# A four-layer graph network: the attention turned by VectorE and a DRAM scratch, dots against a row in PSUM, layer 3's statistics on ScalarE

## The chip, the core and the metric

The kernel runs on one core of a Trainium2 chip. The metric is device time in microseconds (us), the median of several runs. A profile of one further execution shows every instruction. The engines are TensorE (PE; PEld is its weight load), VectorE (DVE), ScalarE (ACT), GpSimd (POOL) and SyncE (SP), which issues DMAs.

## What is computed

x is 128 graphs of 128 nodes with 512 features, adj one 128 x 128 matrix with weights for all of them, all in float32. Four layers follow one another; each ends with `x = layernorm(x + layer(x))` over the 512 features.

```python
# layer 0
out = einsum('bnd,do->bno', einsum('nm,bmd->bnd', adj, x), W0) + bias
# layer 1: q, k, v = x Wq^T, x Wk^T, x Wv^T
rel = adj.T * einsum('bnd,bmd->bnm', q, k)
out = einsum('bnm,bmd->bnd', rel / norm(rel, axis=2), v)
# layer 2: h = x W2, s1 = h a[:512], s2 = h a[512:]
e = leaky_relu(s1[:, :, None] + s2[:, None, :], 0.2) * adj
out = elu(einsum('bij,bjf->bif', softmax(e, axis=2), h) + beta * h)
# layer 3: A = adj x, C = adj x + b
out = max(relu(A[:, :, None, :] + (C - A)[:, :, :, None]), axis=-1)
```

In layer 3 C - A is b for every node, so the layer's output is one number per node, relu(max over features of A + b), which is added to all of that node's features.

## The kernel before, in words

The 128 graphs are worked on in 32 groups of four (`G`, `NG`). Nodes lie on the partitions, so one graph is a tile of 128 x 512. All constants stay in SBUF: `m_qk` is Wq^T Wk, `wa` holds W2 a1 and W2 a2 as two rows spread over all partitions (so that s1 and s2 are dots of x with these rows), `beta_i` is beta times the identity matrix.

**The four large products** (y in layer 0, m and v in layer 1, z in layer 2) are done by a Strassen-Winograd scheme of seven block products instead of eight. `left_factors` makes four sums of blocks of the left matrix on POOL (`s_y`, `s_x`, `s_z`; two of the four overwrite a block where `keep` is 0). `product` emits the seven steps in `ORDER = (1, 2, 6, 5, 7, 3, 4)`; each step is four matmuls of 256 columns that accumulate in one of three PSUM regions r0, r1, r2 (`REGION`). After each step `out(i)` copies (ACT) or adds (DVE) the region to its block of the result. Step 2 writes r1, which out(2) reads; step 5 begins r2. In the y product all seven outs are DVE additions onto x.

**Other PE work of a group**: aggregation of y (`p_y`, four graphs), scores (`p_rel`), attention of layer 1 (`p_o`), spread of the dots (`p_s`), transposes of the attention of layer 2 (`p_eT`), gathering of layer 2 (`p_z`), layer 3's aggregation (`p_a`, called widen).

**Layer 2's attention**: `spread` turns the dots d into rows in PSUM; `leaky` (two DVE instructions) makes e; `weighted` multiplies by adj (POOL); `greatest` takes the maximum (DVE); `exps` are four exponentials with sums (ACT); `divide` takes the reciprocal (DVE) and multiplies (POOL); `turn_att` are four PE transposes; `with_beta` adds beta_i while it copies from PSUM (DVE); `gather` multiplies x by the result. In layer 1 the turned relT and, from the third group on, xT are made otherwise: DVE turns 32 x 32 blocks and DMAs move the blocks within SBUF.

**Order.** Every piece is emitted with a number, and all pieces are sorted by it; each engine then executes its instructions in that order, waiting where data or a buffer is not ready, and runs ahead of the numbers where they are. A group's numbers are those of `TABLE` plus 28 per group, so that four groups are in work at a time; one unit (a slot) is 2.48 us. `LAST` replaces the numbers of the last three groups, `FIRST` some of the first two. Within one period of 28 slots (numbers modulo 28) PE does the m product of one group among the aggregations of the next, then the spread (5.6) of the group before, the y product (7 to 13, with `out` 0.72 after each step) among the scores, v among the gathers, and z among the attention of layer 1 and the widen of an older group.

**Buffers.** [...] four for the tag `ps` (all of `bank()`), four in rotation for the regions r.

## Time and profile before

| what | value |
|---|---|
| median of 10 runs | 2236.58 us (2232.23 to 2244.3) |
| the profiled execution | 2239.64 us, of which 2237.3 are the span from the first instruction to the last |
| PE busy | 2183.0 us, 98% of the span |
| DVE busy | 1797.6 us, 80% |
| ACT, POOL busy | 980.5 and 981.8 us, 44% each |
| DMA engines | 20% busy, 115 MB moved |
| mean granted TensorE clock | 0.996 of full speed |

The profile gives, for groups of equal instructions, engine, operation, output<-inputs, shapes and count, then the busy time and the mean length in ns of one, then the idle time of the engine just before them and what ended it. A matmul in float32 appears as two instructions (passes), a PE transpose as one. Matmuls overlap, so that the length of one is more than the distance from start to start. A line of the waits names who waited for whom, the total in us, how often, and the longest. A line of the timeline gives start, length, engine and instruction; like neighbours are merged (x4). Nearly all lines carry L26, the line of a helper, so that the tile's name tells the place.

### The profile page before, as it was taken

How to read it: one execution, taken by the hardware profiler on the slowest of the kernel's cores; microseconds unless marked ns; L12 is line 12 of the kernel's file. 1: busy time of each engine (PE TensorE's matmuls, PEld its weight loads, DVE VectorE, ACT ScalarE, POOL GpSimd, SP SyncE). 2: the span in 40 equal slices, each digit the busy share in tenths (PEclk: the TensorE clock that was granted, in tenths of full speed). 3: DMA queues.
4: the chain of work that ended last, by engine and by line, in shares of the span. 5: the costliest groups of instructions: out<-in, count | busy, mean ns of one | idle time of the engine just before them, and what ended most of it. 6: DMA issues, size and time to landing. Idle time of an engine off the chain costs nothing.

```text
span 2237.3 us, 31661 instructions
## 1 busy us (share of the span) xinstructions
PE 2183.0 (98%) x11073; PEld 1842.2 (82%) x11073; DVE 1797.6 (80%) x3534; ACT 980.5 (44%) x1936; POOL 981.8 (44%) x743
## 2 busy tenths in 40 slices
PE   7999999999999999999999999999999999999986
PEld 5888888888888888888888888888888888888863
DVE  4668888878878788888788888788888788887787
ACT  2224443444444444444444444444444444344535
POOL 3434455335455344544344553344553344543331
PEclk9999999999999999999999999999999999999998
DMA  4010222211222201222212222202222202221101
GB/s 166 25 42 12 57 57 62 62 36 32 61 59 62 62 17 50 58 60 62 46 29 55 57 62 62 50 24 56 57 62 62 47 25 56 58 62 43 23 25 56
DMA packets 333293, 115.13 MB, mean 51 GB/s; under 512 B 297424, under 2 KB 297552, under 8 KB 333136
## 3 DMA queue, kind: packets, MB, share of 16 engines
q1 hardware_dynamic: 331936, 110.77, 19.7%
q10 hardware_dynamic: 1200, 2.36, 0.3%
q8 instruction: 88, 1.44, 0.3%
q14 instruction: 69, 0.57, 0.1%
HBM read 39.65 MB, written 33.55 MB: 33 GB/s over the span
## 4 chain that ended last, share of the span: by engine, by line
PE 76%; DVE 19%; issue 3%; POOL 1%; ACT 1%; DMA 0%; DVEq 0%; ACTq 0%; POOLq 0%
PE r_v L26 17%; PE r_y L26 15%; PE r_z L26 14%; PE r_m L26 8%; DVE x L26 6%; DVE scr L26 6%; PE p_z L26 5%; PE p_o L26 5%; PE p_a L26 5%; PE p_rel L26 4%; DVE st L26 2%; PE p_y L26 2%; DVE tT L26 1%; DVE d L26 1%; PE p_m L26 1%
## 5 line engine op out<-in xcount | busy, mean ns | idle before, releaser
L26 ACT ACTIVATE x<-x,nmean,rstd 128x512 f32<-128x512 f32 x512 | 385.7, 807 | 187.6 <-DVE nmean L26 187.5
L26 DVE BATCH_NORM_STATS2 st<-x 128x6 f32<-128x512 f32 x512 | 352.0, 688 | 56.7 <-ACT x L26 47.9
L26 DVE SCALAR_TENSOR_TENSOR scr<-x,wa 128x512 f32<-128x512 f32 x256 | 286.3, 1169 | 0.0
L26 POOL TENSOR_TENSOR rstd<-ve,mhalf 128x4 f32<-128x4 f32 (+1 forms) x134 | 145.1, 1083 | 288.7 <-DVE ve L26 282.4
L26 POOL TENSOR_TENSOR x<-x,bias_sb 128x512 f32<-128x512 f32 x128 | 191.7, 1508 | 75.9 <-PE p_y L26 75.1
L26 POOL TENSOR_TENSOR s_x<-xT 128x512 f32<-128x512 f32 x64 | 96.6, 1510 | 259.1 <-DMA xT<-xB 238.5
L26 ACT ACTIVATE x<-x,top 128x512 f32<-128x512 f32 x128 | 92.4, 722 | 229.0 <-DVE top L26 228.8
L26 DVE TENSOR_TENSOR x<-r_y,x 128x512 f32<-128x512 f32 x224 | 151.4, 676 | 25.3 <-PE r_y L26 25.2
L26 ACT COPY c<-r_z 128x512 f32<-128x512 f32 x124 | 71.9, 580 | 221.5 <-PE r_z L26 221.5
L26 ACT COPY yT<-p_y 128x512 f32<-128x512 f32 x128 | 75.2, 587 | 206.0 <-PE p_y L26 206.0
L26 PEld LDWEIGHTS p_y<-adjT,x 128*128 128x128 f32 x1024 | 135.4, 194 | 13.4 <-ACT adjT L26 5.4
L26 DVE SCALAR_TENSOR_TENSOR x<-p_o,rn,x 128x512 f32<-128x512 f32 x128 | 95.9, 749 | 59.9 <-PE p_o L26 56.0
L26 PE MATMUL p_y<-adjT,x 128*128 128x128 f32 x1024 | 136.2, 278 | 6.6 <-ACT adjT L26 5.1
L26 PEld LDWEIGHTS p_z<-eT,x 128*128 128x128 f32 x1024 | 135.3, 193 | 8.4 <-DVE x L26 1.2
L26 DVE SCALAR_TENSOR_TENSOR x<-m,x 128x512 f32<-128x512 f32 x128 | 129.7, 1013 | 13.6 <-DVE x L26 0.9
L26 PEld LDWEIGHTS p_rel<-xT,tT 128*128 128x128 f32 x1024 | 134.1, 191 | 7.4 <-DVE tT L26 0.8
L26 POOL TENSOR_TENSOR s_z<-zT 128x512 f32<-128x512 f32 x31 | 39.3, 1267 | 224.1 <-ACT zT L26 224.1
L26 PE MATMUL p_z<-eT,x 128*128 128x128 f32 x1024 | 136.3, 277 | 0.4 <-DVE x L26 0.4
L26 PE MATMUL p_rel<-xT,tT 128*128 128x128 f32 x1024 | 134.9, 275 | 0.6 <-DVE tT L26 0.6
L26 PE MATMUL p_a<-x,adjT 128*128 128x512 f32 x256 | 131.2, 597 | 3.6 <-ACT x L26 1.9
L26 ACT COPY tT<-r_m 128x512 f32<-128x512 f32 x128 | 75.6, 590 | 133.5 <-PE r_m L26 133.5
L26 PE MATMUL p_o<-v,relT 128*128 128x512 f32 x256 | 130.3, 593 | 0.0
(119 smaller groups left out, 5008.7 us busy)
## 6 DMA issues: line engine op xcount, KB each, us to landing
out_dram<-x SPq DMA_DIRECT2D x128, 256.0 KB, 2.5
x<-in_x_dram SPq DMA_DIRECT2D x31, 1024.0 KB, 5.9
xT<-xB SPq DMA_DIRECT2D x480, 64.0 KB, 2.3
relT<-relB SPq DMA_DIRECT2D x512, 16.0 KB, 1.8
w_sb<-in_L_gnn_weight_dram ACTq DMA_DIRECT2D x1, 1024.0 KB, 6.0
x<-in_x_dram SPq DMA_DIRECT2D x4, 256.0 KB, 7.7
wq_sb<-in_L_gnn_Wq_dram SPq DMA_DIRECT2D x1, 1024.0 KB, 11.9
wk_sb<-in_L_gnn_Wk_dram SPq DMA_DIRECT2D x1, 1024.0 KB, 14.9
```

Of the source, the lines that this page charges most:

```text
L26: return lambda *args, **kw: self.tc.keep_in_program_order(op(*args, **kw))
```

## The change

Seven things are changed. (1) `wa` stays in two PSUM banks, where the PE transposes put it; the two copies to SBUF fall away and the dots read PSUM. (2) To make room, `ps` has three banks instead of four; r0 has two banks of its own, and r1 and r2 share one (`r12`). (3) In groups 0 to 29 `divide` is four DVE instructions that multiply by the reciprocal and add beta_i at once; `turn_blocks` turns 32 x 32 blocks in one DVE instruction, and `move` writes these 256 KB to a DRAM scratch in one DMA and reads them back in four, as eT. The last two groups keep the PE transposes. (4) In layer 3 the sum of squares comes from ACT's squares and the sum from the accumulator of ACT's addition; the ReLU of the maximum is ACT's too; five small DVE instructions make mean and variance. (5) The third and fourth bias addition (POOL) come behind the first two sums of y instead of ahead of them. (6) The third and fourth elu, and layer 3 with them, come some slots later. (7) The numbers around these places are set anew.

```diff
+    psum = ctx.enter_context(tc.tile_pool(name="psum", bufs=1, space=bass.MemoryType.PSUM))
+    dram = ctx.enter_context(tc.tile_pool(name="dram", bufs=2, space=bass.MemoryType.DRAM))
     def bank(name):
+        return psum.tile([P, D], FP, tag="ps", name=name, bufs=3)
...
-    wa = const.tile([P, 2, D], FP)
+    wa = psum.tile([P, 2, D], FP, tag="wa", name="wa")
...
     TABLE = dict(
-        load=[-20], y=row(0.5, 1), bias=row(1.3, 1), y_sums=row(5.2, 0.5), y_w=row(7, 1, 7),
+        load=[-20], y=row(0.5, 1), bias=[4.1, 4.6, 9.1, 9.6],
+        y_sums=[6.8, 7.35, 10.2, 10.75], y_w=row(7, 1, 7),
...
-        residual=row(51.0, 1), dots=row(54.2, 1.1), norm1=[55.2], scale=[58.8],
+        residual=row(51.0, 1), dots=[51.7, 53.8, 54.9, 55.6], norm1=[54.6], scale=[57.2],
...
-        spread=[61.6], leaky=[62.0], weighted=[63.4], greatest=[64.3], exps=[64.4],
-        divide=[65.8], turn_att=[68.6], with_beta=[69.0], gather=row(71.5, 1),
-        z_sums=row(75.3, 0.5), z_w=row(77, 1, 7), exp=[87.5, 88.5, 90.4, 92.0],
-        elu=[87.8, 89.4, 92.8, 93.8], norm2=[95.0], apply2=row(95.7, 0.33),
-        widen=[98.7, 100.0, 103.6, 104.6], top=[99.1, 100.4, 104.0, 105.0],
-        stats3=[99.8, 101.1, 104.7, 105.7], norm3=[106.2], apply3=row(107, 0.33), store=[108.5],
+        spread=[61.6], leaky=[61.6], weighted=[62.3], greatest=[63.0], exps=[63.1],
+        divide=[64.2], turn_att=[68.6], with_beta=[69.0], turn_blocks_2=[64.8], move_2=[64.9], gather=row(71.5, 1),
+        z_sums=row(75.3, 0.5), z_w=row(77, 1, 7), exp=[86.0, 87.0, 96.0, 99.6],
+        elu=[86.4, 87.4, 96.8, 100.3], norm2=[101.4], apply2=row(102.4, 0.33),
+        widen=[104.2, 104.9, 105.6, 106.3], top=[104.7, 105.4, 106.1, 106.8],
+        norm3=[107.4], apply3=row(108.4, 0.33), store=[109.8],
...
             first = i in (1, 2, 5)
             if first:
-                r[where] = psum.tile([P, 2, H], FP, tag="r", name=f"r{where}_{name}")
+                r[where] = psum.tile(
+                    [P, 2, H], FP, tag="r0" if where == 0 else "r12",
+                    name=f"r{where}_{name}", bufs=2 if where == 0 else 1,
+                )
...
         def divide(i):
             rs = small.tile([P, n], FP, tag=f"rs{n}", name=f"rs_{g}_{i}")
             dve.reciprocal(rs, s["sums"][:, i * n : i * n + n])
+            if not late:                       # late = g >= NG - 2
+                for b in range(G):
+                    e = s["e"][:, b, :]
+                    dve.scalar_tensor_tensor(
+                        e, e, rs[:, b : b + 1], beta_i, op0=ALU.mult, op1=ALU.add
+                    )
+                return
...
+        def turn_blocks():
+            s["eB"] = work.tile([P, Q, G, P // Q], FP, tag="eB", name=f"eB_{g}")
+            dve.transpose(
+                s["eB"].rearrange("p q b u -> p b q u"),
+                s["e"].rearrange("p b (q u) -> p b q u", q=Q),
+            )
+
+        def move():
+            m = P // Q
+            blocks = dram.tile([P, Q, G * m], FP, tag="eB", name=f"eBd_{g}")
+            sync.dma_start(blocks, s["eB"].rearrange("p q b u -> p q (b u)"))
+            eT = work.tile([P, Q, G, m], FP, tag="eT", name=f"eT_{g}")
+            for q in range(Q):
+                sync.dma_start(
+                    eT[q * m : (q + 1) * m].rearrange("p a b u -> p a (b u)"),
+                    blocks.rearrange("(a j) q n -> q j a n", a=Q)[q],
+                )
...
+        def squares(b):
+            scr = work.tile([P, D], FP, tag="scr3", name=f"scr3_{g}_{b}")
+            act.activation(scr, x3[g][:, b, :], AF.Square, accum_out=s["sq"][:, b : b + 1])
+
         def top(b):
             dve.tensor_reduce(mx, s["a", b], AX.X, ALU.max)
-            dve.tensor_scalar(tp, mx, b3_sb, 0.0, op0=ALU.add, op1=ALU.max)
-            act.activation(x, x, AF.Identity, bias=tp)
+            act.activation(tp, mx, AF.Relu, bias=b3_sb)
+            act.activation(x, x, AF.Identity, bias=tp, accum_out=s["sum"][:, b : b + 1])
+
+        def spread(i):      # mean, and var = sq/D + EPS - (mean of x before the addition)^2
+            dve.tensor_scalar(s["mean", i], s["sum"][:, sl], -1.0 / D, None, op0=ALU.mult)
+            dve.tensor_tensor(d, s["mean", i], s["top"][:, sl], ALU.add)
+            dve.scalar_tensor_tensor(d, d, -1.0, d, op0=ALU.mult, op1=ALU.mult)
+            dve.tensor_scalar(s["sq"][:, sl], s["sq"][:, sl], 1.0 / D, EPS, op0=ALU.mult, op1=ALU.add)
+            dve.tensor_tensor(d, d, s["sq"][:, sl], ALU.add)
+            pool.tensor_tensor(s["r"][:, sl], d, mhalf[:, sl], ALU.pow)
...
-        each(t["stats3"], lambda b: stats(s, f"3_{g}", b, x3[g][:, b, :]))
-        norm(t["norm3"], t["apply3"], s, f"3_{g}", lambda: x3[g])
+        each(t["norm3"], spread)
```

## The prediction

> **What bounds the kernel now.** I read the page's engine table first, then the chain, then the groups by form on PE and DVE, PE's waits, and last the timeline around one group's attention.

> ```profile
> span 2237.3 us, 31661 instructions
> PE 2183.0 (98%) x11073; PEld 1842.2 (82%) x11073; DVE 1797.6 (80%) x3534; ACT 980.5 (44%) x1936; POOL 981.8 (44%) x743
> PE 76%; DVE 19%; issue 3%; POOL 1%; ACT 1%; DMA 0%; DVEq 0%; ACTq 0%; POOLq 0%
> ```

> TensorE (PE) is busy 98% of the span and carries the chain; VectorE (DVE) at 80% only takes it at the end. So time falls where PE issues less or waits less, and rises where PE waits more. In the timeline the four spread transposes `p_s`, one set per group, start 66.81 us apart in the shortest interval; the 28 intervals between the second group and the thirtieth average 67.75. The shortest is PE without a wait: by start-to-start times a group is 112 matmuls of the products at 2 passes of 0.216 (48.4), 48 of 128 columns at 2 passes of 0.112 (10.7), 8 of 512 columns at 2 passes of 0.429 (6.9) and 8 transposes at 0.109 (0.9), together 66.8. About 0.94 us a group is waiting:

> ```profile
> PE r_m L26 <- DVE tT L26: 8.8, 6, 1.7
> PE r_y L26 <- DVE x L26: 4.8, 18, 0.4
> PE p_eT L26 <- DVE rs L26: 2.2, 2, 1.7
> ```

> All of these are DVE being late, and the groups by form show one reason: an instruction with two SBUF inputs takes 1.0 to 1.2 us in the mean, one with a PSUM input 0.75.

> ```profile
> L26 DVE SCALAR_TENSOR_TENSOR scr<-x,wa 128x512 f32<-128x512 f32 x256 | 286.3, 1169 | 0.0
> L26 DVE SCALAR_TENSOR_TENSOR x<-p_o,rn,x 128x512 f32<-128x512 f32 x128 | 95.9, 749 | 59.9 <-PE p_o L26 56.0
> L26 PE MATMUL p_eT<-ident,e 128*128 128x128 f32 x128 | 20.0, 275 | 2.2 <-DVE rs L26 2.2
> ```

> The first timeline is PE through one attention, the second DVE and POOL at a place where short DVE instructions meet a busy POOL.

> ```profile
> 1199.55 0.60 PE L26 MATMUL p_s<-ident,d 128*128 128x128 f32 x4
> ...
> 1201.72 3.62 PE L26 MATMUL r_y<-w_sb,yT 128*128 128x256 f32 x16
> 1205.17 1.05 PE L26 MATMUL p_rel<-xT,tT 128*128 128x128 f32 x8
> 1206.06 1.89 PE L26 MATMUL r_y<-t,s_y 128*128 128x256 f32 x8
> 1207.79 1.05 PE L26 MATMUL p_rel<-xT,tT 128*128 128x128 f32 x8
> 1208.68 1.89 PE L26 MATMUL r_y<-w_sb,s_y 128*128 128x256 f32 x8
> ```

> ```profile
> 1934.94 1.85 DVE L26 SCALAR_TENSOR_TENSOR d<-mv,wa_sum,d 128x4 f32<-128x4 f32 x2
> 1936.89 1.13 DVE L26 TENSOR_TENSOR d<-d,rstd 128x8 f32<-128x8 f32 x1
> 1932.36 5.64 POOL L26 TENSOR_TENSOR x<-x,bias_sb 128x512 f32<-128x512 f32 x4
> ```

> See in the first: step 5 of the y product (the last line) starts 9.13 us after the spread. In the second, three tiny instructions, 0.17 to 0.21 us elsewhere, take 3.0 us: behind back-to-back POOL instructions of 1.27 us each, one DVE instruction gets through per POOL instruction.

> [...] 0.68 alone and up to 1.75 us beside POOL for `scr<-x,wa`, while `x<-p_o,rn,x` keeps 0.75. [...]

> **The change, part by part.**

> *Attention's transposes.* Groups 0 to 29 lose four PE transposes: 120 x 0.109 = **-13.1 us**, all on the path. With them go the copy with beta (0.67 on DVE) and the POOL division (1.04).

> *Dots, layer 3, elu.* `wa` in PSUM takes 8 dots a group from 1.17 to about 0.75 (-3.4 us DVE); layer 3 drops 4 bn_stats and 4 aggregates (4 x 0.87) and the 0.21 us tops, adding about 1.3 us of small instructions; ACT gains 4 squares, 4 accumulator reads and 4 ReLUs, about 5 us a group (nearest rows: 0.72, 0.19; ReLU of one column not shown, 0.2 to 0.4). ACT was 30.6 of 69.4 us a period, so PE's 66 cover it. If that cover were gone, the cost would be a later x3 and so a later widen: up to 0.5 us a group. DVE, some 5 us lighter a group, and two of four elus moved away from the m product: the waits named above should nearly all go. Of 28 x 0.94 = 26.5 I take **-25** (bounds -12 to -26.5). Fewer PSUM buffers (ps 3, r12 one) make new waits possible; in my order of work the banks are free at least 1 us ahead, but for the one place below.

> *Edges.* The chain's last 40 us are mostly DVE: elu, statistics, tops. The eight bn_stats pairs of the last two groups go (8 x 0.8 = 6.4), their tops' 8 x 0.13 too, and about 2.5 of small norm3 work comes: -5; the first two groups wait for DVE about 4 us at `d` and `tT`: -3. Together **-8** (0 to -12; ACT's extra work at the end could eat it).

> *The scratch.* SP gets one write and four reads more a group. Issues take 0.59 us (relT's median), the store lands in 2.5, xT's 64 KB in 2.3. From the turned blocks: 0.6 + 2.5, then 4 x 0.6 + 2.3 = 7.8 us, in which relT's sixteen issues (and any load behind) wait on SP; they are needed 9 slots later. The gather starts about 21 us after the spread; the blocks are turned at 12.4 (below), eT is there at 20.2 and PE will itself be late by then. Cost 0 (bounds 0 to 1 us a group).

> *The new wait.* This decides. `divide` is now four instructions e = e*rs + beta_i on DVE, both tensors in SBUF, emitted ahead of out(2) of the y product (8.2 against 8.72 in slots). With r12 a single buffer, step 5 (r2) cannot start until out(2) has read r1. Times from the spread's start, durations from the timeline around 1200 us: leaky starts at 0.64, two instructions, to 2.05; POOL's product with adj 2.13 to 3.40; maximum 0.72; four exps 1.65, to 5.80; reciprocal, then the first division asks at about 6.03. POOL meanwhile runs on: two y sums to 5.98, and as the third and fourth bias now stand behind these, bias from 5.94, then bias, sum, sum, each 1.27, to 10.90. By the one-for-one rule the four divisions end near 7.25, 8.5, 9.7 and 10.95. out(2) takes 0.68 more and PE 0.14 to start: 11.82 against 9.13 wanted, **+2.7 us** a group, 30 x 2.7 = **+81**. A 128x128 form of this instruction is not in the trace; its neighbour (`e<-e,rs`) is 0.29 with POOL idle, and four of them without POOL would end at 6.9: the other bound is 0. Queued behind PE's wait are two score blocks, the rest of y, then v; behind the divisions on DVE out(2), the turn and out(6).

> Sum: -13.1 - 25 - 8 + 81 = +35. The profiled execution took 2239.64 (span 2237.3), so 2274.5; it lies 3.1 above the median of the runs, so **2272**.

> **Rivals.**
> 1. *The divisions pass POOL* (two or more per gap, or a short form not held up). Then step 5 waits 0 to 0.6 us and the sum is -46 to -28: 2190 to 2209. For it: in most groups the second of the three `d` instructions slipped through when POOL's next came over 0.1 us late. Against it: here POOL's queue is full. It decides from a wait below 1.5 us a group.
> 2. *The first division gets in ahead of the third bias.* The two requests are 0.09 us apart (6.03 and 5.94). One POOL instruction less: 1.4 us a group, 42 in all, sum -4: 2233, no change.
> 3. *More than I see*: the divisions' wait and also an eT that is late by 1 us: +30, about 2300. The trace shows slack against it.

> **How the numbers follow.** Forecast 0.50, with its own range 2256 to 2287 (wait 2.7 +- 0.3, edges and old waits +- 8); rival 1: 0.34; rival 2: 0.13, split about evenly between the three outcomes; rival 3: 0.03. That gives faster by over 0.2% 0.38, within 0.2% (about 4.5 us, what a measurement of this kernel can tell from no change) 0.05, slower 0.57. Two in ten lie outside 2194 to 2287.

> **What would show it.** In the profile after: four PE transposes fewer in each of 30 groups; `scr<-x,wa` at 0.75; `e<-e,rs,beta_i` near 1.2 us instead of 0.3, one per POOL instruction; a PE wait "r_y <- DVE x" at step 5 of y of some 2.7 us times 30, spreads 69.1 us apart. A division at 0.3 us and spreads below 67 us would prove me wrong; waits of `p_z` for eT would prove rival 3.

## The result and the profile after

The kernel takes 2321.36 us after the change (median of 9 runs, 2317.86 to 2321.76) against 2236.9 before: 1.0375 times as long (95% interval 1.0362 to 1.0387). The direction and the place were forecast; the forecast of 2272 with a range to 2287 was 49 us too low. The profiled span is 2320.8 us, 83.5 more than before.

The page's head, engine table and chain, and then two of PE's waits:

```profile
span 2320.8 us, 32156 instructions
PE 2204.1 (95%) x10953; PEld 1857.4 (80%) x10953; DVE 1661.4 (72%) x3410; ACT 1097.0 (47%) x2446; POOL 866.9 (37%) x713
PE 80%; DVE 11%; ACT 4%; issue 2%; POOL 2%; DMA 0%; ACTq 0%; DVEq 0%
```

```profile
PE r_y L26 <- DVE x L26: 76.5, 30, 2.9
PE r_m L26 <- DVE tT L26: 3.5, 1, 3.5
```

DVE, POOL and the DMAs are not short of time: DVE is 136 us less busy than before. Yet PE has one large new wait (`r_y`), once in each of the 30 groups that divide on DVE. And a second thing stands in the engine table: PE issues 120 instructions fewer and is busy 21 us longer, so some matmuls must have become slower.

The groups by form, first DVE's, then PE's:

```profile
L26 DVE SCALAR_TENSOR_TENSOR scr<-x,wa 128x512 f32<-128x512 f32 x256 | 162.4, 681 | 0.0
L26 DVE SCALAR_TENSOR_TENSOR e<-e,rs,beta_i 128x128 f32<-128x128 f32 x120 | 153.6, 1338 | 1.1
L26 PE MATMUL r_y<-w_sb,s_y 128*128 128x256 f32 x512 | 140.1, 422 | 76.5 <-DVE x L26 76.5
L26 PE MATMUL p_eT<-ident,e 128*128 128x128 f32 x8 | 1.9, 300 | 2.2 <-DVE rs L26 2.2
```

The dots went from 1169 to 681 ns, better than the 0.75 us assumed. The divisions take 1338 ns each, four times the 344 ns that a run below shows where POOL does not hold them. Step 5 of y (`r_y<-w_sb,s_y`, together with step 3, which has the same name) went from 382 ns (in the profile before) to 422 in the mean. One attention in the timeline of after; DVE, POOL and PE one after another:

```profile
1179.31 0.18 DVE L26 RECIPROCAL rs<-sums 128x4 f32<-128x4 f32 x1 [1.06 <-ACT e L26]
1179.52 5.11 DVE L26 SCALAR_TENSOR_TENSOR e<-e,rs,beta_i 128x128 f32<-128x128 f32 x4
1184.56 0.68 DVE L26 TENSOR_TENSOR x<-r_y,x 128x512 f32<-128x512 f32 x1
1179.40 2.54 POOL L26 TENSOR_TENSOR x<-x,bias_sb 128x512 f32<-128x512 f32 x2
1181.91 1.31 POOL L26 TENSOR_TENSOR yT<-yT 128x512 f32<-128x512 f32 x1
1183.18 1.30 POOL L26 TENSOR_TENSOR s_y<-yT,s_y 128x512 f32<-128x512 f32 x1
1173.46 0.60 PE L26 MATMUL p_s<-ident,d 128*128 128x128 f32 x4
1181.70 1.05 PE L26 MATMUL p_rel<-xT,tT 128*128 128x128 f32 x8
1185.29 3.34 PE L26 MATMUL r_y<-w_sb,s_y 128*128 128x256 f32 x8 [2.53 <-DVE x L26]
1188.42 1.43 PE L26 MATMUL p_rel<-xT,tT 128*128 128x128 f32 x8
```

The divisions begin 0.12 us after the third bias and end with the fourth POOL instruction: 5.11 us for four. out(2) follows, and step 5 starts 11.83 us after the spread (1185.29 less 1173.46); 11.82 had been worked out. But step 5 then takes 3.34 us where 1.89 is usual, and the scores 1.43 where 1.05 is. The table by stage shows why (columns: length, busy times with counts, granted TensorE clock, DMA share, GB/s); its rows are the stretch before the wait, the wait, and two behind it:

```profile
1173.50:1182.60 9.10, 9.10 (x53) 8.24 (x51) 6.58 (x9) 2.23 (x9) 6.92 (x6) 1.00 0.00 1
1182.60:1185.30 2.70, 0.17 (x3) 0.01 (x1) 2.70 (x4) 0.00 (x0) 1.88 (x2) 1.00 0.00 0
1185.78:1189.19 3.41, 3.41 (x11) 2.81 (x11) 1.18 (x4) 3.26 (x5) 0.00 (x0) 0.50 0.26 94
1189.19:1195.00 5.81, 5.81 (x35) 5.29 (x34) 3.27 (x9) 1.47 (x9) 0.41 (x1) 1.00 0.13 38
```

The granted clock is 0.50, half of full speed, for the 3.41 us that begin 0.5 us after the wait's end. Measured from start to start, the matmuls of the 28 groups between the second spread and the thirtieth lose 2.70 us a group in the wait and 1.26 in passes slower than their usual spacing. In 17 of those groups a half-clock stretch follows the wait, and the slow passes cost 1.9 us; in the others they cost only 0.1 to 0.4.

### The profile page after: what moved, and what is told of

It reads as the page before. It is cut to its first block, busy times and chain, and to the rows that moved or that the text cites. A ratio compares the mean times of both kernels' runs of the same rounds, so it can differ in the third digit from the quotient of the medians.

```text
span 2320.8 us, 32156 instructions
## 1 busy us (share of the span) xinstructions
PE 2204.1 (95%) x10953; PEld 1857.4 (80%) x10953; DVE 1661.4 (72%) x3410; ACT 1097.0 (47%) x2446; POOL 866.9 (37%) x713
## 4 chain that ended last, share of the span: by engine, by line
PE 80%; DVE 11%; ACT 4%; issue 2%; POOL 2%; DMA 0%; ACTq 0%; DVEq 0%
PE r_v L26 16%; PE r_z L26 16%; PE r_m L26 14%; PE r_y L26 11%; DVE e L26 7%; PE p_y L26 5%; PE p_z L26 5%; PE p_o L26 5%; PE p_a L26 4%; PE p_rel L26 3%; ACT e L26 2%; DVE x L26 2%; POOL e L26 2%; DVE nm L26 1%; ACT x L26 1%
## 5 line engine op out<-in xcount | busy, mean ns | idle before, releaser
L26 ACT ACTIVATE x<-x,nmean,rstd 128x512 f32<-128x512 f32 x384 | 285.6, 807 | 211.0 <-DVE nmean L26 207.5
L26 DVE BATCH_NORM_STATS2 st<-x 128x6 f32<-128x512 f32 x384 | 263.2, 685 | 8.8
L26 DVE TENSOR_TENSOR x<-r_y,x 128x512 f32<-128x512 f32 x224 | 153.0, 683 | 136.5 <-PE r_y L26 133.1
L26 POOL TENSOR_TENSOR rstd<-ve,mhalf 128x4 f32<-128x4 f32 (+1 forms) x99 | 108.9, 1100 | 336.3 <-DVE ve L26 336.3
L26 PE MATMUL r_y<-w_sb,s_y 128*128 128x256 f32 x512 | 140.1, 422 | 76.5 <-DVE x L26 76.5
L26 POOL TENSOR_TENSOR x<-x,bias_sb 128x512 f32<-128x512 f32 x128 | 172.2, 1357 | 60.5 <-PE p_y L26 60.5
L26 PEld LDWEIGHTS r_y<-w_sb,s_y 128*128 128x128 f32 x512 | 99.9, 205 | 95.0 <-DVE x L26 82.2
L26 ACT COPY yT<-p_y 128x512 f32<-128x512 f32 x128 | 75.1, 587 | 200.0 <-PE p_y L26 200.0
L26 DVE TENSOR_REDUCE mx<-p_a 128x1 f32<-128x512 f32 x128 | 88.3, 691 | 104.9 <-PE p_a L26 102.2
L26 DVE SCALAR_TENSOR_TENSOR scr<-x,wa 128x512 f32<-128x512 f32 x256 | 162.4, 681 | 0.0
L26 PEld LDWEIGHTS p_rel<-xT,tT 128*128 128x128 f32 x1024 | 148.6, 209 | 9.7 <-DVE tT L26 0.8
L26 DVE SCALAR_TENSOR_TENSOR e<-e,rs,beta_i 128x128 f32<-128x128 f32 x120 | 153.6, 1338 | 1.1
L26 ACT ACTIVATE x<-x,mean,r 128x512 f32<-128x512 f32 x128 | 97.1, 807 | 111.3 <-DVE mean L26 111.3
L26 PE MATMUL p_rel<-xT,tT 128*128 128x128 f32 x1024 | 147.9, 292 | 0.6 <-DVE tT L26 0.6
L26 PEld LDWEIGHTS p_y<-adjT,x 128*128 128x128 f32 x1024 | 138.7, 199 | 12.0 <-ACT adjT L26 5.6
L26 POOL TENSOR_TENSOR e<-e,adj_sb 128x512 f32<-128x512 f32 x32 | 40.7, 1272 | 286.7 <-DVE e L26 281.5
L26 ACT COPY tT<-r_m 128x512 f32<-128x512 f32 x128 | 75.6, 590 | 150.1 <-PE r_m L26 150.1
L26 PE MATMUL p_y<-adjT,x 128*128 128x128 f32 x1024 | 139.5, 282 | 5.3 <-ACT adjT L26 5.3
L26 PEld LDWEIGHTS p_z<-eT,x 128*128 128x128 f32 x1024 | 135.4, 193 | 7.9 <-issue 1.0
L26 POOL TENSOR_TENSOR rn<-n,mhalf 128x4 f32<-128x4 f32 x32 | 32.6, 1017 | 291.4 <-ACT sq L26 291.4
L26 PE MATMUL p_z<-eT,x 128*128 128x128 f32 x1024 | 136.3, 277 | 0.0
L26 PE MATMUL p_a<-x,adjT 128*128 128x512 f32 x256 | 125.5, 593 | 5.8 <-DVE mx L26 4.4
```

The lines of the kernel that those rows point to most:

```text
L26: return lambda *args, **kw: self.tc.keep_in_program_order(op(*args, **kw))
```

## The experiments

The theory after this reading: one division gets through per POOL instruction, as in the timeline above, where four took 5.11 us beside four of POOL (I call this the hold); out(2), behind them, is late; r12 has one buffer, so step 5 waits; and the wait slows TensorE. Its rivals: too few PSUM banks; small divisions that are slow in themselves; slow passes caused by DMAs or DVE; layer 3 on ScalarE.

**The hold alone.** The divisions read beta_i from PSUM. To make room, one row of W2 goes back to SBUF.

```diff
-                        e, e, rs[:, b : b + 1], beta_i, op0=ALU.mult, op1=ALU.add
+                        e, e, rs[:, b : b + 1], beta_p, op0=ALU.mult, op1=ALU.add
```

> Only the place of beta_i and of one of the two rows changes: the divisions read beta_i from PSUM, so they have one SBUF tensor input; one row of wa moves back to SBUF to make room. Order, counts and banks of ps, r0 and r12 are as after. Theory (the divisions are held up by POOL, one per POOL instruction, and step 5 waits for out(2)): the four divisions take about 0.3 us each, out(2) ends near 7.6 us after the spread, step 5 needs it at 9.1, so the wait of 2.7 and the slow TensorE passes after it vanish in 30 groups: 2321 - 30 x (2.7 + 1.26) = about 2202 us. Rival (too few PSUM banks cost the time) and rival (128x128 divisions with a pointer scalar are slow in themselves): 2321, as after.

Measured: 2204.39 us, 0.9854 of before (0.9835 to 0.9873). The group by form in this kernel:

```profile
L26 DVE SCALAR_TENSOR_TENSOR e<-e,rs,beta_p 128x128 f32<-128x128 f32 x120 | 33.7, 344 | 1.1
```

The same 120 instructions, in the same place behind the same POOL work, take 344 instead of 1338 ns, and 117 us are gone. The single r12 bank and the three ps banks are still there: they cost nothing by themselves in the steady groups, where spreads are 66.51 us apart. The first rival falls. The second falls with the next run: here one input has moved to PSUM, there both are in SBUF.

**POOL's queue shorter.** Only the biases go back ahead of the sums.

```diff
-        bias=[4.1, 4.6, 9.1, 9.6]
+        bias=row(1.3, 1)
```

> Only the four bias additions go back to their old numbers (1.3 to 4.3), ahead of the sums of y. Theory: two POOL instructions are left behind the second sum instead of four; two divisions get through at their ends, the last two at once, out(2) ends about 9.6 us after the spread, step 5 waits 0.6 us: 2321 - 30 x (3.96 - 0.6) = about 2220 us, 2202 to 2235. Rival (PSUM banks): 2321. Rival (the wait comes from the reordered attention alone, wherever POOL works): 2321.

Measured: 2229.98 us, 0.9968 of before (0.9953 to 0.9982), wait 0.68 us in each group. The timeline of DVE, then of POOL:

```profile
1133.07 3.10 DVE L26 SCALAR_TENSOR_TENSOR e<-e,rs,beta_i 128x128 f32<-128x128 f32 x4
1132.96 1.27 POOL L26 TENSOR_TENSOR yT<-yT 128x512 f32<-128x512 f32 x1
1134.19 1.31 POOL L26 TENSOR_TENSOR s_y<-yT,s_y 128x512 f32<-128x512 f32 x1
```

With two POOL instructions left, two divisions are held (1.30 and 1.35 us by the trace) and the last two take 0.34. That is again one division per POOL instruction, and at 0.34 us divisions with both inputs in SBUF are not slow in themselves.

**The order on DVE.** The divisions stay slow, but go behind out(2), the turn behind out(6).

```diff
-        divide=[64.2], ..., turn_blocks_2=[64.8], move_2=[64.9]
+        divide=[64.74], ..., turn_blocks_2=[65.75], move_2=[65.8]
```

> Only the order on DVE changes: divide comes directly behind out(2) of the y product, the turn of the blocks behind out(6). Theory: the divisions still take about 1.3 us each, but step 5 no longer waits for them; they end at about 11.7 us after the spread, out(6) at 12.4, and step 7 wants it at 11.8, so about 0.7 us of wait remains, too short to slow TensorE: 2321 - 30 x (3.96 - 0.7) = about 2223 us. Rival (the divisions' slowness by itself costs the time, DVE being short): 2310 or more. Rival (banks): 2321.

Measured: 2215.21 us, 0.9896 (0.988 to 0.9912), spreads 66.85 us apart. The group by form:

```profile
L26 DVE SCALAR_TENSOR_TENSOR e<-e,rs,beta_i 128x128 f32<-128x128 f32 x120 | 137.2, 1201 | 1.1
```

The divisions still take 1201 ns in the mean; they cost 0.34 us a group (66.85 against 66.51) where out(2) no longer stands behind them. So the price of the hold is less DVE's time than what stands behind it in the queue.

**The wait filled.** Three matmuls into an unread bank, directly ahead of step 5.

```diff
+        def fill():
+            p = psum.tile([P, D], FP, tag="ps", name=f"p_fill_{g}", bufs=3)
+            for k in range(3):
+                pe.matmul(p, adjT, w0_sb[:, k, :], start=True, stop=True)
+        if g > 1:
+            emit(t["y_w"][3] - 0.1, fill)
```

> Three more matmuls of 128x512 in each of 30 groups, directly ahead of step 5 of y, into a ps bank that nobody reads: 2.6 us of PE work a group, put into the wait of 2.7. Nothing of the result depends on them. Theory (the wait itself halves TensorE's clock for the next 3.4 us): the wait is filled, the clock stays full, the 1.26 us a group of slow passes vanish: 2321 - 38 = about 2283 us, faster although PE does 77 us more. Rival (the slow passes come from something else that runs then, like the block turn's DMAs or DVE): 2321 or a little more. Rival (PE's own amount of work sets the time, the wait is none): about 2398.

Measured: 2286.44 us, 1.0222 of before (1.0203 to 1.024): 35 us faster than after with more work. PE's groups in this kernel:

```profile
L26 PE MATMUL r_y<-w_sb,s_y 128*128 128x256 f32 x512 | 124.2, 385 | 0.3 <-DVE x L26 0.3
L26 PE MATMUL p_fill<-w_sb,adjT 128*128 128x512 f32 x180 | 82.2, 593 | 0.0
```

Step 5 is back at 385 ns, no half-clock stretch remains in the 28 groups (the mean granted clock is 0.997, against 0.981 in after), and the divisions (1340 ns) and the scratch are as after, so neither they nor the DMAs are the cause. The slow passes went when PE's idle time was filled.

**How long a wait does it.** One of the two late biases goes ahead of the sums, so three POOL instructions follow.

```diff
-        bias=[4.1, 4.6, 9.1, 9.6]
+        bias=[4.1, 4.6, 4.7, 9.6]
```

> Only the third bias addition goes back ahead of the sums (4.7), the fourth stays behind them: three POOL instructions follow the second sum, against four after and two in the version with all biases first (2230 us, wait 0.68). Theory: the wait at step 5 is 0.68 + 1.27 = 1.95 us. If a wait of that length still slows TensorE as the wait of 2.7 does: 2230 + 30 x (1.27 + 1.2) = 2304 us. If only waits over some 2 us do: 2230 + 38 = 2268 us. Rival (no one-for-one rule): 2321 or 2230, as its neighbours.

Measured: 2258.66 us, 1.01 (1.0079 to 1.0121). PE's wait at step 5 (this view counts the idle time, 0.17 us less than from start to start):

```profile
PE r_y L26 <- DVE x L26: 46.3, 30, 1.9
```

From start to start the wait is 1.70 us, not 1.95: one more POOL instruction turns a free division (0.34 us) into a held one (1.35), which adds 1.0 us, where I had added a whole POOL instruction of 1.27. None of the 28 groups has a half-clock stretch. So with waits of 0.68 and 1.70 us the mean granted clock was 0.995, about that of before (0.996); with those of 2.70 it was 0.981, and 17 groups of 28 had a half-clock stretch.

Why only 17, the trace of after answers. Its 22 half-clock stretches begin whole multiples of 3.413 us apart, to within 1 ns, as on a fixed grid; the two of before also do (27.30 us apart, eight steps). The groups with a stretch differ from the others in how long PE is idle within one step of this grid. Two waits of after, step by step, with the columns of the table above:

```profile
1182.37:1185.78 3.41, 0.88 (x6) 0.66 (x5) 3.41 (x4) 0.00 (x0) 2.11 (x2) 1.00 0.00 0
407.55:410.97 3.42, 2.41 (x16) 2.04 (x14) 3.42 (x4) 0.00 (x0) 3.42 (x4) 1.00 0.00 0
410.97:414.38 3.41, 1.87 (x9) 1.66 (x10) 2.75 (x5) 1.23 (x2) 0.74 (x1) 1.00 0.13 50
414.38:417.79 3.41, 3.41 (x25) 3.20 (x24) 1.32 (x2) 2.23 (x4) 0.00 (x0) 1.00 0.31 95
```

The first wait lies in one step: PE is busy for 0.88 us of it, idle for 2.53, and the next step is the half-clock one of the table above. The second wait is as long, but the grid cuts it into 1.0 and 1.5 us of idle time, and no step is slow. In the 28 groups PE was idle for 2.03 us or more in the step ahead of each of the 17 slow ones, and for at most 1.95 in any step of the others. Over the whole trace of after (the first 25 us and the last two steps apart), each of the 21 full-clock steps with 2.0 us of idle time or more has a half-clock step behind it, and none with less than 1.9 has; of the two between, one has (1.93 us) and one has not (1.95). The waits of 1.70 us held 1.54 us of idle time in the mean (46.3 in 30 waits). This is read from the traces; no run was made to shift a wait against the grid.

**The attention part undone.**

```diff
-        late = g >= NG - 2
+        late = True
```

> The attention part alone is undone: all 32 groups divide on POOL and turn with PE transposes as the last two do; PSUM, dots, layer 3, biases and all other numbers stay as after. Theory (the attention part costs the wait and the slow passes, and saves 13.1 us of transposes; all else is a gain): no wait at step 5, spreads 66.8 us apart, 13 us above the version with beta_i in PSUM (2204): 2217 us, 2210 to 2224. Rival (PSUM banks or layer 3 on ScalarE cost part of the 84 us): above 2237.

Measured: 2218.2 us, 0.9916 (0.9895 to 0.9938). Everything else in the change together is a gain of 0.8%, so neither the PSUM banks nor layer 3 on ScalarE caused the loss; the attention part turned the gain into a loss of 3.7%.

**The attention part alone, on the kernel before.** The diff is the division, turn and move of the change, with its numbers directly behind out(2):

```diff
+        divide=[64.75], turn_blocks_2=[64.79], move_2=[64.8]
```

> The kernel before, with the attention part alone: divisions with beta_i on DVE, block turn and DRAM scratch for 30 groups, emitted directly behind out(2) of y; four rotating banks for r, rows of W2 in SBUF, biases first. Theory (with POOL's biases done early and r not in one bank, nobody waits for the divisions): the transposes' 13.1 us come off, the older waits of 0.94 us a group stay: 2237 - 13 = 2224, 2215 to 2232. Rival (block turn and scratch are slower for PE than four transposes, because eT is late for the gather): above 2237, with waits of p_z.

Measured: 2323.14 us, 1.0396 (1.0365 to 1.0427): my expectation missed by 99 us, and the rival's reason is not it either, for no matmul of `p_z` waits. The timeline of DVE, then PE:

```profile
1174.07 1.14 DVE L26 SCALAR_TENSOR_TENSOR e<-e,rs,beta_i 128x128 f32<-128x128 f32 x4
1175.24 0.71 DVE L26 STREAM_TRANSPOSE eB<-e 128x512 f32<-128x512 f32 x1
1175.88 0.65 DVE L26 SCALAR_TENSOR_TENSOR x<-c,x 128x512 f32<-128x512 f32 x1
...
1178.16 0.69 DVE L26 TENSOR_TENSOR x<-r_y,x 128x512 f32<-128x512 f32 x1
1178.99 2.39 PE L26 MATMUL r_y<-t,yT 128*128 128x256 f32 x8 [1.99 <-DVE x L26]
```

The four divisions take 1.14 us together, unhindered. But I had put them and the turn ahead of an elu that the old table has there; all of it stands ahead of out(6) on DVE, which step 7 waits for. The waits were 2.1 to 2.9 us from start to start, and 17 of 28 groups again have a half-clock stretch (mean granted clock 0.983). So a loss of the same size arises without the hold, from 1.85 us of divisions and turn put into DVE's queue ahead of an `out` that had no time to spare. It suggests what the later elus of the change are good for: they clear this place. Both are read from the trace; no run moved the pieces.

**Both orders at once**, beta_i left in SBUF (the edits of the second and third experiment together):

> Both orders at once, beta_i left in SBUF: biases ahead of the sums, divisions behind out(2), block turn behind out(6). Theory: two divisions still wait for POOL (1.3 us each), two take 0.35; with out(2) ahead of them they end about 10 us after the spread and out(6) at 10.4, where step 7 wants it at 11.8: nobody waits, spreads 66.4 to 66.5 us apart, as with beta_i in PSUM: 2204 us, 2198 to 2210. Rival [...]: 2215 or more, as with the divisions behind out(2) alone.

Measured: 2205.51 us, 0.9862 (0.9845 to 0.988): numbers in the table alone do what the PSUM copy does.

**A faster version.** Two edits to the one with beta_i in PSUM: the first group's last dot and scaling behind out(2) of the next m product, and the last two groups' layer 3 as before.

```diff
+    FIRST = {0: dict(..., dots=[51.7, 53.8, 54.9, 57.74], scale=[57.8]), ...}
+        old = g >= NG - 2        # layer 3: stats and norm by DVE
```

> The version with beta_i in PSUM (2204.4), with two edits: the first group's last dot and its scaling come behind out(2) of the second group's m product, and the last two groups take layer 3's statistics by DVE as before. Theory: a wait of 3.9 us near 106 us and the slow passes behind it (about 5 us) go, and the last chain is 2 to 3 us shorter: 2204 - 11 = 2193 us, 2188 to 2198. Rival (the early wait is absorbed by a later one; ScalarE isn't what ends last): 2204.

Measured: 2199.7 us, 0.9834 (0.9813 to 0.9855), profiled span 2195.4 against 2202.8. That misses the 2188 to 2198 that I expected. By the trace the second spread comes 6.1 us earlier, not 9: the wait is gone, but the slow passes behind it had cost 2.5 us, not 5. Another 1.6 us are saved at the end. Both versions were compared with the kernel before and not with each other, and the intervals of their ratios overlap: that this one beats the kernel before is shown; that it beats the version it comes from rests on the spans of one profile each.

## Why the prediction was right and wrong

- **Transposes, -13.1**: right. With and without them, and with no new wait, 2218.2 and 2204.4 us.
- **Old waits, -25**: right within its bounds. Without the new wait the spreads are 66.51 us apart, against 67.76 before: 0.44 of that are the transposes, 0.81 the waits, 23 us in 28 groups.
- **The scratch, 0**: right. Its write lands in 2.0 us and its reads in 2.0; no gather waits, so the third rival falls.
- **The new wait, +2.7 a group**: right in place, cause and size (2.70). The third bias does get in first, by 0.12 us, which settles the second rival (its sum should read -7, not -4: 35 less 42); the first is refuted by 1338 ns a division. One division per POOL instruction is what the runs show: in after each of the 120 took 1.29 to 1.36 us, and the POOL instructions beside those of the timeline above 1.26 to 1.31.
- **Edges, -8**: wrong. The second spread comes 9.1 us later than before. One group's wait and slow passes are 4.6 of that (the run with the divisions behind out(2) has this spread 4.6 us earlier). Most of the rest is the single r12 bank: the first group's last dots and scaling, held by POOL's biases, stand ahead of out(2) of m, and that is the 3.5 us of `r_m` above and then 6.83 us at a granted clock of 0.50. From the thirtieth spread to the end it is 1.9 us more, with one group's 4.1 in it: so 2 saved instead of 5, since ScalarE now leads the last chain. Together about +2.
- **What was missing: +35.** This is the step that failed: the sum took a wait to cost its own length. In the 28 groups each cost 3.83 us (spreads 70.34 apart against 66.51), with the first and the last 116 us in all, where 81 had been put. The 1.13 beyond the wait are nearly all half-speed matmuls: 17 groups of 28 lose 1.7 us more in slow passes than the other 11, 1.0 in the mean. This one term, with the edges, is the miss: -13 - 23 + 2 + 81 + 35 = +82 against 83.5 in the spans. The kernel before has a mean granted clock of 0.996, so I passed over the clock; here waits of 2.7 us were enough to bring the mean to 0.981.

Two readings were off without consequence: ACT's 30.6 us belong to a period of 67.8 us, not 69.4, and POOL's four instructions in the second timeline took 1.41 us each (5.64 for four), not 1.27. ScalarE's ReLU of one column took 0.29 us, within the 0.2 to 0.4 assumed for it.

The range's upper end came from the wait's own uncertainty. With these 35 us for what a wait leaves behind, it would just have held the result.

## What to carry to other kernels

The price of a slowed instruction was here what stood behind it in the engine's queue: ahead of the addition that frees a PSUM bank, the divisions at 1.34 us each made PE wait 2.70 us a group; behind it, at 1.2 us each, they cost 0.34 us a group. Before a short instruction with two SBUF inputs is put on DVE, count the POOL instructions queued at that moment: in after each of them held one division for about 1.3 us. And when TensorE bounds a kernel, a wait may cost more than its length: here 1.7 us more in the groups where it left TensorE idle for 2.03 us or more within one 3.413 us step than in the others. Filling it with matmuls whose result nobody reads is a quick test of that.
